# A second tile list ordered by tile number, with the first eight batches gathered and normed inside the expert-tile stage of a two-layer attention and mixture-of-experts kernel

## The chip, the cores and the metric

The kernel runs on one core of one Trainium2 chip. The metric is the device time of one execution in microseconds (us); a kernel is run several times, and the median is compared. The core has a matrix engine (PE; its weight loads are shown as PEld), a vector engine (DVE), a scalar engine with lookup tables (ACT), a general engine (POOL) and a queue engine that issues most transfers (SP). PE writes only to PSUM, which has eight banks of 128 x 512 floats here; everything else works from SBUF, which has 128 partitions.

## The reference, cut to what matters

The input x has 64 batches of 128 tokens of width 128. Two layers follow each other, each an attention and a feed-forward with eight experts:

```
x = x + L0_attention(layernorm(x), fside, ctx)      # 16 heads of width 8; 128 keys from fside and 120 from ctx
x = x + L0_experts(layernorm(x))                    # per token: 8 logits, top 2 experts,
                                                    #   out = sum_k score_k * (silu(a) * g) @ w2[e_k],  a, g = x @ w1[e_k]   (F = 352)
x = x + L1_attention(layernorm(x), ctx)             # 16 heads, 120 keys
x = x + L1_experts(layernorm(x))                    # top 2 of 8 experts, hidden width 64, gelu
```

The token count is 64 x 128 = 8192, so layer 0's experts have 16384 rows of work. The logits of layer 0 depend on the data, so which rows belong to which expert is known only while the kernel runs.

## The kernel before, in words

The whole x stays in SBUF as 16 tiles `xg[g]` of four batches each (a group is GB = 4 batches). There are three stages, one after the other.

Stage 1 is `attention(0, ...)`: a loop over `it`, one new batch per turn, in which a batch's scores, softmax, values and output projection are spread over five turns (so 64 + 5 turns). Beside it the layer-0 router runs (`Router`, called at fixed points of each turn): it norms a group, finds the two experts of each token, and scatters each token's normed row into an array `xs` in HBM, where every expert has its own region of CAP rows, in the order of the tokens. The row that a token got there within all regions is kept in `posns`, the choice of expert as a one-hot in `chosen`.

Stage 2 is `tile_stage`. It works through NTL = 71 tiles of TT = 256 rows of one expert. For each tile, `fetch(t)` reads from a list the expert and the first row into registers of SP (`value`, L851), then issues three transfers (the 256 rows from `xs`, the expert's weights, the scores of the rows). `turn` transposes the rows on PE, `hidden` makes the hidden layer (12 matmul records at L1030, silu on ACT at L1034, product on DVE at L1035), `project` the output (L1043), scales it on DVE (L1049) and writes it from SP into an HBM array `ys` (L1050). Slots rotate over five buffers, and tile t + 3 is fetched while tile t is worked on. `between(t)` puts in small pieces of other work after each tile. There are two lists: "a", for the first NA = 32 tiles, is made when 40 of the 64 batches have been routed, so that stage 2 can begin before the routing is over; "b", for the other 39, is made when all are routed. Both go expert by expert. The generator `lists` makes them, and after them `back`, for every token the two rows of `ys` where its results will stand.

Stage 3 is `attention(1, ...)`. Before it can norm a batch, that batch's two result rows per token must come back from `ys`: `Aside1.fetch` issues two indirect gathers per batch from POOL (L1216), `Aside1.lead` adds them to x on POOL (L1228) and takes the statistics on DVE (L112, L113); POOL then makes the root (`Norm.roots`, L155 to L157) and the normed tile `xn` (L167). In the first turns `prep_batch` transposes one batch at a time (L313), makes its queries (L316, L318), and the score matmuls (L373, and L401 for the second pass) follow; from the second group on `prep_x` (L176) and `prep_q` (L289) do a whole group. `norm_of` makes `xn` of a coming group, and `biased` adds the output bias to x. Four gathers go out in each of the first five turns and two in each later one. Layer 1's experts are in stage 3 as pieces between the turns.

The instructions of PE, ACT, DVE and POOL stand in the order in which the program writes them. SP's transfers are ordered so only in the first turns and from the last two turns of stage 1 on; in the stretch between, a scheduler places them as early as what they depend on allows. Every DMA from SP uses one of eight semaphores in turn, so it waits until the transfer eight before it has landed.

Of the kernel before, what the change touches and what calls it, by code (L numbers as in the profile page):

```python
# [44 lines left out]
def transformer_kernel(ctx, tc, a, out):  # L45
# [186 lines left out]
    def attention(layer, w, norm, first, aside):  # L232
# [5 lines left out]
        with ExitStack() as es:  # L238
# [278 lines left out]
            for it in range(B + 5):  # L517
                def on(back, *steps):
                    b = it - back
                    if 0 <= b < B:  # L520
                        for f in steps:
                            f(b)

                def rounds(*which):
                    ba = it if it < B else None
                    bc = it - 2 if 0 <= it - 2 < B else None
                    for r in which:
                        if ba is not None or bc is not None:
                            round_(ba, bc, r)

                if first and it % GB == 2:
                    norm_of(it // GB + 2)
                if 2 <= it <= B + 1:
                    ps_[it - 2] = work.tile([128, nc_, 4, 512], F32, name="p", tag="p")
                if it % GB == 0 and 0 < it // GB + 1 < NG:
                    if it:
                        loads(it // GB + 1)
                vals = (lambda b: values(b, 0), lambda b: values(b, 1), out1)
                if first:
                    rounds(0, 1)  # L540


                    on(5, out4)
                    on(1, shift)
                    on(5, out5)
                    aside.ahead(it)
                    aside.call(it, mtile)
                    on(3, *vals)
                    if it % GB == 2 and it // GB + 1 < NG:
                        context(it // GB + 1)  # L550
                    prep(it, 0)
                    aside.call(it, mtile)
                    rounds(2, 3)
                    on(4, out3)
                    on(3, out2)
                    prep(it, 1)
                    aside.end(it, work, mtile)
                else:
                    on(3, *vals)
                    rounds(0, 1)  # L560


                    aside.piece(mtile)
                    if it < GB - 1:
                        prep_batch(it + 1)
                    prep(it, 0)
                    on(4, out3)
                    on(3, out2)
                    on(5, out4)
                    aside.call(it, mtile)  # L570
                    prep(it, 1)
                    on(1, shift)
                    on(5, out5)
                    aside.ahead(it)
                    if it == GB - 1 or it > GB and it % GB == 1:
                        norm_of(it // GB + 1)
                    if it == 1:
                        biased(0)
                    if it == GB - 1:
                        prep_x(1)  # L580
                        prep_q(1, 0)
                        prep_q(1, 1)
                    aside.fetch_for(it)
                    aside.call(it, mtile)
                ps_.pop(it - 3, None)
                yield
# [259 lines left out]
        return lists_.tile(shape, dt, name=name, tag=name)  # L846

    TILES = {}

    def value(ap, most):  # L850
        return nc.values_load(  # L851
# [25 lines left out]
    def tile_list(name, n, begin, off):  # L877
# [28 lines left out]
        TILES[name] = te_i, tr_i  # L906
        yield

    def lists():
        while len(filled) < GA // 2:  # L910
            yield
# [13 lines left out]
        in_a, cut = small("in_a", [S, E]), small("cut", [S, 1 + E])  # L925
        nc.vector.tensor_scalar(cut, begin_a, float(NA), None, ALU.min)
        nc.vector.tensor_tensor(in_a, cut[:, 1:], cut[:, :E], ALU.subtract)
        nc.vector.tensor_tensor(nt, nt, in_a, ALU.subtract)
        begin_b = summed(nt, "b")
        yield  # L930
        off, two = small("off_b", [S, E]), small("two", [S, E])
        nc.vector.tensor_tensor(two, in_a, begin_b[:, :E], ALU.subtract)
        nc.vector.scalar_tensor_tensor(off, two, float(TT), first_row, ALU.mult, ALU.add)
        top_i = small("top_i", [1, E], I32)
        nc.vector.tensor_copy(top_i, top[0:1, :])
        TILES["top"] = top_i
        yield
        yield from tile_list("b", NTL - NA, begin_b, off)

        first, more, move = small("first", [S, E]), small("more", [S, E]), small("move", [S, E])  # L940
        nc.vector.scalar_tensor_tensor(first, in_a, float(TT), first_row, ALU.mult, ALU.add)
        nc.vector.scalar_tensor_tensor(move, begin_a[:, :E], float(TT), first_row, ALU.mult, ALU.subtract)

        nc.vector.tensor_tensor(more, two, begin_a[:, :E], ALU.add)
        nc.vector.tensor_scalar(more, more, float(NA), -float(TT), ALU.subtract, ALU.mult)
        for k in range(2):
            got = []
            for n, col in enumerate((first, move, more)):
                yield
                prod, by = small("prod", [S, B, E]), small(f"by_{n}", [S, B])  # L950
                nc.vector.tensor_tensor(
                    prod, chosen[:, k], col.unsqueeze(1).to_broadcast([S, B, E]), ALU.mult
                )
                yield
                nc.vector.tensor_reduce(by, prod, AX.X, ALU.add)
                got.append(by)
            yield
            at_, move_, more_ = got
            nc.vector.tensor_tensor(at_, posns[:, k], at_, ALU.is_ge)
            nc.vector.tensor_tensor(more_, more_, at_, ALU.mult)  # L960
            nc.vector.tensor_tensor(move_, move_, more_, ALU.add)
            nc.vector.tensor_tensor(back[:, :, k], move_, posns[:, k], ALU.add)


    SLOTS = 5

    def tile_stage(work, mtile):


        w_of, x_of, xT_of, hT_of, share_of, y_of = {}, {}, {}, {}, {}, {}  # L970
        probes = [None]
        zeros_left = list(range(E))

        def slot(t):
# [5 lines left out]
            return s.rearrange("p b h i w -> p (b h i w)")  # L980

        def fetch(t):
            name, u = ("a", t) if t < NA else ("b", t - NA)
            te_i, tr_i = TILES[name]
            e = value(te_i[:, u : u + 1], E - 1)
            r = value(tr_i[:, u : u + 1], E * CAP - TT)
            s = slot(t)
            n = NF * 3 * 128
            w = s[:, :n].rearrange("p (c f) -> p c f", c=NF)
# [48 lines left out]
        def project(t):  # L1038
# [8 lines left out]
            y, share = y_of.pop(t), share_of.pop(t)  # L1047
            for h in range(2):
                nc.vector.tensor_scalar(y[:, h, :], po[:, h, :], share[:, h, :], None, ALU.mult)  # L1049
            nc.sync.dma_start(ys[t * TT : (t + 1) * TT].rearrange("(h p) d -> p h d", p=S), y)  # L1050
            probes.append(y[0:1, 0, 0:1])

        def between(t):

# [3 lines left out]
                    rt.call(probes[-1], mtile)  # L1058
            elif zeros_left and "top" in TILES:
                zeros(zeros_left.pop(0))  # L1060
            next(aside0.steps, None)
            if t == NA:
                kvT = work.tile([D, GB, KF], F32, name="kvT", tag="kvT")
                kvT = kvT.rearrange("d b k -> d (b k)")[:, : GB * KC]
                kvT = kvT.rearrange("d (b k) -> d b k", b=GB)
                nc.sync.dma_start(kvT, a["ctxT"][:, 0:GB, :])
                probes[0] = kvT
            if t == NA + 6:
                keys_of(l1, probes[0], 0, KC, mtile())
            if t == NA + 10:  # L1070
                values_of(l1, probes[0], 0, KC, mtile())

        for t in range(2):
# [5 lines left out]
        for t in range(NTL):  # L1079
# [5 lines left out]
            if t + 3 < NTL:  # L1085
                if t + 3 == NA:
                    assert len(filled) == NG // 2 and not zeros_left
                    for _ in aside0.steps:
                        pass
                fetch(t + 3)  # L1090
            if t > 2:
                between(t)
# [14 lines left out]
    class Aside0(Ahead):  # L1107
# [28 lines left out]

        def end(self, it, work, mtile):

            if it == B - 2:
                self.tiles = tile_stage(work, mtile)  # L1140
            if it >= B - 2:
# [37 lines left out]
    wr1 = load_const("wgT", [D, E], a["wgT"])  # L1179
    bg = load_row("bg", E)  # L1180
    lw1 = load_const("lw1T", [D, E * R], a["lw1T"])
    steps256 = load_row("steps256", CAP // TT)
    tiles = load_const("tiles", [1, NTL], a["tiles"])
    select = load_const("select", [128, 4, 128], a["select"])
    lw2 = load_const("lw2T", [128, 4, D], a["lw2T"].rearrange("(c p) d -> p c d", p=128))
    with tc.manual_schedule(engines=ORDERED):
# [7 lines left out]
    class Aside1:  # L1194


        def __init__(self, pool):
            self.pool, self.got, self.b, self.xn = pool, {}, 0, None
            self.xnTs, self.gates, self.ready = {}, [], []
            for k in range(2):  # L1200
                t = pool.tile([S, QM, 32], F32, name=f"gates_{k}", tag=f"gates_{k}")
# [20 lines left out]
        def lead(self, b):  # L1222
# [4 lines left out]
                for k in range(2):  # L1227
                    nc.gpsimd.tensor_tensor(x, x, y[:, k], ALU.add)  # L1228
            norms[2].stats(b)
            if b < GB:  # L1230
                if b % 2:
                    norms[2].roots(b - 1, b + 1)
                    self.xn = norms[2].normed(0, xn=self.xn, js=(b % GB - 1, b % GB))
            elif b % GB == GB - 1:
                norms[2].roots(b + 1 - GB, b + 1)

        def normed(self, j):
# [5 lines left out]

        def ahead(self, it):

            for b in ((2, 3), (), (4, 5), (6, 7), (8, 9), (10, 11))[it] if it < 6 else (it + 6,):
                if b < B:
                    self.lead(b)

        def fetch_for(self, it):  # L1250
            self.fetch(2 if it < 5 else 1)

        def xnT_of(self, g):
            self.xnTs[g] = self.pool.tile([D, GB * S], F32, name="xnT", tag="xnT", bufs=4)
# [74 lines left out]

    with ExitStack() as es:  # L1330
        aside1 = Aside1(es.enter_context(tc.tile_pool(name="yb", bufs=1)))
        aside1.fetch(3)
        aside1.lead(0)
        aside1.lead(1)
        aside1.fetch(1)
        with tc.manual_schedule(engines=ORDERED):
            for _ in attention(1, l1, norms[2], False, aside1):
                pass
# [2 lines left out]
def _laid_out(inp):  # L1341
# [57 lines left out]
    for e in range(E):  # L1399
        t[:, e, e // 2, e % 2, :] = 1.0  # L1400
    o["select"] = t.reshape(128, 4, 128)
    o["tiles"] = np.arange(NTL, dtype=np.float32).reshape(1, -1)
    o["first_row"] = np.arange(E, dtype=np.float32) * CAP
    o["wgT"] = A["L1_ffn_Wg"].T
    o["bg"] = A["L1_ffn_bg"]
# [21 lines left out]
```

## Time and profile before

| what | value |
|---|---|
| median of 3 runs | 1624.24 us (1620.74 to 1625.42) |
| the profiled execution's own time | 1627.08 us |
| its span, first to last instruction | 1625.1 us, mean granted PE clock 0.954 |
| PE busy in 0 to 600 us (stage 1) | about 96 to 99% after the first 100 us |
| PE busy in 640 to 980 us (stage 2) | 310.45 of 340 us |
| PE busy in 980 to 1060 us (start of stage 3) | 49.44 of 80 us, granted clock 0.68 |
| PE busy in 1060 to 1560 us (rest of stage 3, without its end) | about 93% |
| DVE busy in stage 2 | 159.47 of 340 us |
| DMA share in stage 2 | 0.62 of 16 engines, 181 GB/s |

Two views are used most. A table of windows gives for each stretch the busy time of each engine with the number of instructions, then the granted PE clock (1.00 is full speed), the share of the 16 DMA engines that was busy, and the GB/s moved. A list of waits gives, for each engine and line, the engine and line that ended the wait, the total of the waits, how many there were and the longest. In a timeline, a row is start, duration, engine, line, operation and tiles, and in brackets the idle time ahead of it and what ended it.

### The profile page before, as it was taken

The page shows a single profiled execution, that of the slowest core. Times are in us where ns is not written, and L with a number is a line of the kernel's source. Part 1 is how long each engine was busy: PE and PEld are TensorE (multiplying, and loading weights), DVE is VectorE, ACT ScalarE, POOL GpSimd, SP SyncE. Part 2 cuts the span into 40 slices and gives each one's busy share as a digit, 9 for nine tenths or more (in the row PEclk, how much of TensorE's full clock was granted, in tenths as well). Part 3 has the DMA queues.
Part 4 walks back from the last instruction along what each step waited for, and adds up shares of the span by engine and source line. Part 5 has one row for each costly group of instructions (what it writes and reads, how often), then busy time and mean ns, then how long its engine had stood idle before and what let it go on. Part 6 is the DMA issues. An engine that isn't in the chain of part 4 may idle for free.

```text
span 1625.1 us, 44888 instructions
## 1 busy us (share of the span) xinstructions
PE 1489.3 (92%) x18162; PEld 1184.0 (73%) x18162; DVE 1072.5 (66%) x2935; ACT 842.1 (52%) x1739; POOL 642.3 (40%) x1198
## 2 busy tenths in 40 slices
PE   7999999999999998879999994788999999999997
PEld 5777777777777676768888883567777777777775
DVE  6778888888889883545544442477666656667763
ACT  4666666666566564423333332455555555555553
POOL 4123355656565344640000005575554555443200
PEclk9999999999999998999999996799998989899999
DMA  8311122222222211667666651110001111000000
GB/s 211 84 45 45 45 58 60 59 58 74 58 64 71 65 51 59 181 175 207 198 193 189 192 172 43 29 36 25 27 27 36 29 30 30 29 27 15 10 13 26
DMA packets 124129, 123.88 MB, mean 76 GB/s; under 512 B 47123, under 2 KB 106515, under 8 KB 122003
## 3 DMA queue, kind: packets, MB, share of 16 engines
q1 hardware_dynamic: 115730, 103.71, 23.2%
q0 software_dynamic: 8192, 17.32, 3.4%
q8 instruction: 143, 2.34, 0.6%
q14 instruction: 64, 0.52, 0.1%
HBM read 97.31 MB, written 23.67 MB: 74 GB/s over the span
## 4 chain that ended last, share of the span: by engine, by line
PE 74%; DVE 11%; DMA 4%; issue 3%; ACT 3%; POOL 3%; SPq 1%; another core or an unknown queue 0%; POOLq 0%; DVEq 0%; ACTq 0%
PE bank L401 13%; PE bank L373 12%; PE bank L1030 9%; PE bank L446 9%; PE bank L1305 4%; PE bank L1284 3%; DVE nm L385 3%; PE bank L1043 3%; PE bank L289 2%; DMA q<-xs 2%; PE bank L1294 2%; PE bank L482 2%; PE bank L202 2%; PE bank L214 2%; PE bank L653 2%
## 5 line engine op out<-in xcount | busy, mean ns | idle before, releaser
L385 DVE TENSOR_REDUCE nm<-bank 128x2 f32<-128x496 f32 (+1 forms) x768 | 465.2, 663 | 151.0 <-PE bank L401 89.6
L401 PE MATMUL bank<-q,k 32*120 32x256 f32 (+1 forms) x3072 | 480.4, 408 | 16.8 <-issue 5.6
L373 PE MATMUL bank<-k,q 32*128 32x248 f32 (+1 forms) x4096 | 466.0, 345 | 11.1 <-issue 7.5
L409 ACT ACTIVATE p<-bank 120x512 f32<-120x512 f32 (+1 forms) x768 | 402.4, 603 | 138.0 <-PE bank L401 102.8
L373 PEld LDWEIGHTS bank<-k,q 32*128 32x128 f32 x4096 | 355.5, 191 | 80.4 <-issue 32.9
L401 PEld LDWEIGHTS bank<-q,k 32*120 32x120 f32 (+1 forms) x3072 | 302.2, 181 | 47.2 <-DVE nm L385 16.1
L446 PE MATMUL bank<-p,v 128*32 128x128 f32 (+1 forms) x4096 | 178.4, 278 | 4.6 <-DVE nm L385 4.0
L1035 DVE TENSOR_TENSOR p<-p,bank 128x256 f32<-128x256 f32 x213 | 88.2, 420 | 139.5 <-ACT p L1034 126.4
L784 POOL DMA_INDIRECT xs<-xn,at x128 | 129.3, 1010 | 28.5 <-issue 24.9
L455 ACT COPY ov<-bank 128x256 f32<-128x256 f32 x128 | 47.9, 374 | 176.1 <-PE bank L446 130.9
L1216 POOL DMA_INDIRECT yb<-ys,back x128 | 124.0, 968 | 32.2 <-issue 24.6
L1034 ACT ACTIVATE p<-bank 128x256 f32<-128x256 f32 x213 | 80.9, 384 | 102.4 <-PE bank L1030 97.1
L446 PEld LDWEIGHTS bank<-p,v 128*32 128x32 f32 (+1 forms) x4096 | 110.8, 110 | 29.6 <-issue 15.9
L1030 PE MATMUL bank<-q 128*128 128x256 f32 x516 | 122.3, 388 | 3.0 <-ACT oT L477 3.0
L433 DVE SCALAR_TENSOR_TENSOR q<-bank,c_smask,q 128x256 f32<-128x256 f32 x256 | 111.2, 476 | 14.2 <-PE bank L430 10.9
L167 POOL TENSOR_SCALAR xn<-x,mv,rstd 128x128 f32<-128x128 f32 x252 | 110.6, 451 | 6.2
L155 POOL TENSOR_SCALAR rstd<-mv 128x4 f32<-128x4 f32 (+1 forms) x33 | 6.6, 199 | 268.0 <-DVE mv L113 181.2
L293 ACT ACTIVATE q<-bank,c_a_bq,c_hmask 128x512 f32<-128x512 f32 x120 | 87.3, 785 | 47.7 <-PE bank L289 47.7
L1030 PEld LDWEIGHTS bank<-q 128*128 128x128 f32 x516 | 97.4, 196 | 15.6 <-ACT oT L477 3.4
L446 PE MATMUL bank<-p,vc 120*32 120x128 f32 x2048 | 104.2, 272 | 0.5 <-issue 0.5
L1202 POOL MEMSET gates<- 128x256 f32 x2 | 0.6, 312 | 251.3 <-DMA ys<-q 251.3
L138 POOL TENSOR_TENSOR mv<-st 128x4 f32<-128x4 f32 x31 | 6.4, 207 | 195.4 <-DVE st L109 195.4
(205 smaller groups left out, 2412.5 us busy)
## 6 DMA issues: line engine op xcount, KB each, us to landing
q<-in_w SPq DMA_DIRECT2D x43, 576.0 KB
vc<-in_w SPq DMA_DIRECT2D x28, 576.0 KB
vc<-in_ctx_v SPq DMA_DIRECT2D x16, 960.0 KB
k<-in_ctx_k SPq DMA_DIRECT2D x32, 240.0 KB
q<-xs SPq DMA_DIRECT2D x43, 128.0 KB
ys<-q SPq DMA_DIRECT2D x43, 128.0 KB
x<-in_x SPq DMA_DIRECT2D x16, 256.0 KB
kvT<-in_fsideT SPq DMA_DIRECT2D x16, 256.0 KB
```

Of the source, the lines that this page charges most:

```text
L167: nc.gpsimd.tensor_scalar(xn[:, j, :D], xg[g][:, j, :], self.mv[:, b, 0:1], self.rstd[:, b : b + 1], ALU.add, ALU.mult,)
L293: nc.scalar.activation(q4s[g][:, :, s, :], pq.rearrange("p (b q) -> p b q", b=GB), AF.Identity, bias=w["bq"][:, s : s + 1], scale=hmask[:, ...
L373: nc.tensor.matmul(pa[:, u, :], lhsT=q4s[g][r, j, s, :], rhs=k2[g % 2][r, s // 2, j, :], start=True, stop=True,)
L385: nc.vector.tensor_reduce(nm[b % 2].rearrange("q i (a s) -> q a i s", s=16)[:, 2 * ra + v : 2 * ra + v + len(slots) // 2, :, 0], pa.rearra ...
L401: nc.tensor.matmul(pb[:n, v * 256 : (v + 1) * 256], lhsT=k2[g % 2][r, v, j, k0 : k0 + n], rhs=q4s[g][r, j, 2 * v : 2 * v + 2, :].rearrange ...
L409: nc.scalar.activation(ps_[b][:n, c, ra, :], pb[:n], AF.Exp, scale=SCALE)
L433: nc.vector.scalar_tensor_tensor(q, pm, smask[:, v : v + 1], q, ALU.mult, ALU.add)
L446: nc.tensor.matmul(pav[32 * ra : 32 * ra + 32, v * S : (v + 1) * S], lhsT=vs[g % 2][c][:, j, 4 * v + ra, i, :], rhs=p[:n, c, ra, (2 * v + ...
L784: s = nc.gpsimd.indirect_dma_start(xs, bass.IndirectOffsetOnAxis(at[:, j, k : k + 1], 0), xn, None)
L1030: nc.tensor.matmul(ph[:, u, :], lhsT=w[:, c, u * 128 : (u + 1) * 128], rhs=xT, start=True, stop=True)
L1035: nc.vector.tensor_tensor(hT[:, c, :], sa, ph[:, 1, :], ALU.mult)
L1216: nc.gpsimd.indirect_dma_start(y[:, k, b % 2, :], None, ys, bass.IndirectOffsetOnAxis(back[:, b, k : k + 1], 0),)
```

## The change

The change has four parts.

First, list "b" is made in another order: by a tile's number within its expert, then by expert. `tile_list_by_number` works on all 128 partitions at once (264 = 33 x 8 possible tiles per partition), marks those that list "a" left over, numbers them with a scan, and each partition picks out the tile of its own number; so the list stands down the partitions, one tile in each, instead of along one partition. `back` follows the new order by a longer formula.

Second, `first_results` gathers, adds and norms the first eight batches while the last tiles are worked on. The rows of batches 2u and 2u + 1 are within the first 256(u + 1) rows of each expert, so their results stand in `ys` once list "a" and the first 8(u + 1) tiles of list "b" are written. It begins after tile 41, with one step per tile and eight tiles per pair of batches.

Third, stage 3 begins with those two groups normed (`READY`): its gathers start at batch 8, two batches in the first turn and one in each later turn.

Fourth, each of the 71 tiles of `ys` is filled with zeros from SP during stage 1, so that a gather never reads a row that was not written.

Beside these, `between` takes two steps of the list's generator per tile instead of one once list "b" is there, and the keys and values of stage 3's first group are made two and four tiles earlier.

```diff
@@ attention, second layer
-                    if it == GB - 1 or it > GB and it % GB == 1:
+                    if it > GB and it % GB == 1:
                         norm_of(it // GB + 1)
-                    if it == 1:
-                        biased(0)
                     if it == GB - 1:
+                        normed[1] = READY[1]
                         prep_x(1)
@@ lists
+    def tile_list_by_number(s, n):
+        shape = [S, U, E]
...
+        nc.vector.tensor_tensor(one, u, s256.unsqueeze(1).to_broadcast(shape), ALU.is_ge)
+        nc.vector.tensor_tensor(at, n256.unsqueeze(1).to_broadcast(shape), u, ALU.is_gt)
+        nc.vector.tensor_tensor(one, one, at, ALU.mult)
+        nc.vector.tensor_tensor_scan(at_, one_, nothing, 0.0, ALU.add, ALU.add)
+        nc.vector.tensor_tensor(at_, at_, one_, ALU.mult)
+        nc.vector.tensor_scalar(at_, at_, row_number[:, 0:1], None, ALU.is_equal)
...
+        nc.vector.tensor_tensor(one, at, order.unsqueeze(1).to_broadcast(shape), ALU.mult)
+        nc.vector.tensor_reduce(te, one_, AX.X, ALU.add)
+        nc.vector.tensor_tensor(one, at, u, ALU.mult)
+        nc.vector.tensor_reduce(tr, one_, AX.X, ALU.add)
...
+        TILES["b"] = te_i, tr_i
@@ lists(), the rows of back, for each of the two choices k
-            for n, col in enumerate((first, move, more)):
+            for n, col in enumerate((first, move, order)):
                 yield
                 prod, by = ...
                 nc.vector.tensor_tensor(prod, chosen[:, k], col..., ALU.mult)
                 yield
                 nc.vector.tensor_reduce(by, prod, AX.X, ALU.add)
...
+            nc.vector.tensor_tensor(prod, order..., o..., ALU.is_gt)
+            yield
+            nc.vector.tensor_tensor(prod, prod, u.unsqueeze(2).to_broadcast(wide), ALU.add)
+            nc.vector.tensor_tensor(prod, prod, in_a.unsqueeze(1).to_broadcast(wide), ALU.max)
+            yield
+            nc.vector.tensor_tensor(prod, prod, nt.unsqueeze(1).to_broadcast(wide), ALU.min)
+            nc.vector.tensor_reduce(u, prod, AX.X, ALU.add)
...
@@ tile_stage
         def fetch(t):
-            name, u = ("a", t) if t < NA else ("b", t - NA)
+            te_i, tr_i = TILES["a" if t < NA else "b"]
+            u = (slice(0, 1), slice(t, t + 1)) if t < NA else (slice(t - NA, t - NA + 1), slice(0, 1))
...
+        def first_results(t):
+            u, step = divmod(t - NA - E - 1, E)
+            if not 0 <= u < 4:
+                return
+            if step == 0:
+                y = work.tile([D, GB, KF], F32, name="kvT", tag="kvT")
...
+                needed = written[NA : NA + E * (u + 1)]
+                for b in range(2):
+                    for k in range(2):
+                        g = nc.gpsimd.indirect_dma_start(
+                            y[:, k, b, :], None, ys,
+                            bass.IndirectOffsetOnAxis(back[:, 2 * u + b, k : k + 1], 0),
+                        )
...
+                        behind(g, needed)
+            elif step == 1:
...
+                for k in range(2):
+                    nc.gpsimd.tensor_tensor(x, x, y[:, k], ALU.add)
+            elif step == 2:
+                for b in range(2):
+                    norms[2].stats(2 * u + b)
+            elif step == 3 and u % 2:
+                g = u // 2
+                norms[2].roots(g * GB, g * GB + GB)
+                READY.append(norms[2].normed(g))
+            elif step == 4 and u % 2:
+                nc.gpsimd.tensor_tensor(xg[g], xg[g], l1["bo"]..., ALU.add)
...
-            next(aside0.steps, None)
+            for _ in range(2 if "b" in TILES else 1):
+                next(aside0.steps, None)
+            if t == NA + E:
+                for _ in aside0.steps:
+                    pass
+            first_results(t)
...
+            if t == NA + 4:
+                keys_of(l1, probes[0], 0, KC, mtile())
             if t == NA + 6:
-                keys_of(l1, probes[0], 0, KC, mtile())
-            if t == NA + 10:
                 values_of(l1, probes[0], 0, KC, mtile())
@@ Aside0.end, each turn of stage 1
+            for t in range(2 * (it - GB), 2 * (it - GB) + 2):
+                if 0 <= t < NTL:
+                    nc.sync.dma_start(
+                        ys[t * TT : (t + 1) * TT].rearrange("(h p) d -> p h d", p=S), zero[:, :, :D]
+                    )
@@ Aside1
-            self.pool, self.got, self.b, self.xn = pool, {}, 0, None
+            self.pool, self.got, self.b, self.xn = pool, {}, 2 * GB, READY[0]
...
-            for b in ((2, 3), (), (4, 5), (6, 7), (8, 9), (10, 11))[it] if it < 6 else (it + 6,):
+            for b in ((), (8,), (9,), (10,), (11,), ())[it] if it < 6 else (it + 6,):
...
-            self.fetch(2 if it < 5 else 1)
+            self.fetch(2 if it == 0 else 1)
@@ start of stage 3
         aside1 = Aside1(es.enter_context(tc.tile_pool(name="yb", bufs=1)))
-        aside1.fetch(3)
-        aside1.lead(0)
-        aside1.lead(1)
-        aside1.fetch(1)
```

## The prediction

> **What bounds the kernel now.** I read the page first, for where PE loses time.
>
> ```profile
> PE   7999999999999998879999994788999999999997
> POOL 4123355656565344640000005575554555443200
> PEclk9999999999999998999999996799998989899999
> L1202 POOL MEMSET gates<- 128x256 f32 x2 | 0.6, 312 | 251.3 <-DMA ys<-q 251.3
> ```
>
> PE is at nine tenths nearly everywhere; the hole is in the slice from 975 us, where its clock is low too. POOL is empty for some 250 us before it, waiting for `ys` (the row of L1202). So the tiles run at PE's pace, POOL has room in them, and the start of stage 3 is bound by something else. The windows from 930 us on, busy times in the order PE, PEld, DVE, ACT, POOL, SP, then clock, DMA share, GB/s:
>
> ```profile
> 975.00:980.00 5.00, 1.91 (x18) 1.72 (x16) 1.33 (x5) 0.00 (x0) 0.10 (x1) 1.00 0.18 52
> 980.00:985.00 5.00, 0.00 (x0) 0.00 (x0) 0.00 (x0) 0.00 (x0) 3.90 (x6) 0.56 0.43 134
> 995.00:1000.00 5.00, 4.10 (x32) 3.51 (x34) 0.73 (x2) 1.77 (x5) 1.07 (x2) 0.50 0.00 0
> 1030.00:1035.00 5.00, 3.21 (x6) 1.23 (x6) 0.00 (x0) 0.59 (x1) 4.47 (x8) 0.50 0.00 0
> ```
>
> PE stops at 976.9, comes back at 995 at half clock, and POOL is the busy engine between. The chain that ended last gives the order (start, duration, what), the list of waits from 975 to 1070 the totals (total, count, longest):
>
> ```profile
> 976.95 0.62 DVE q L1049 x2
> 977.59 1.83 DMA ys<-q
> 979.89 0.56 POOL gates L1202 x2
> 983.23 2.43 DMA yb<-ys,back
> 994.51 0.45 POOL xn L167
> 995.00 0.49 PE bank L313
> 997.17 3.57 PE bank L373 x29
> ```
> ```profile
> PE bank L313 <- POOL xn L167: 18.1, 1, 18.1
> DVE st L112 <- POOL x L1228: 17.5, 2, 14.3
> PE bank L176 <- POOL xn L167: 5.1, 1, 5.1
> ACT p L409 <- remote: 3.8, 1, 3.8
> ```
>
> One serial path: last write, gathers, sums, statistics, root, `xn`, transposes. PE's waits after it (5.1 at L176) are the same chain for later batches.
>
> **Cost of the zeros.** In the order of the changed program, SP's 71 fills are not spread over stage 1: they stand together, eight behind the second group's kvT, one more kvT, then 63, all ahead of the next group's k, vc and kvT. Before, SP had free time there:
>
> ```profile
> 37.83 1.34 SPq L255 DMA_DIRECT2D kvT<-in_fsideT  x2
> 62.71 0.93 SPq L260 DMA_DIRECT2D k<-in_ctx_k  x2
> 81.65 0.47 PE L373 MATMUL bank<-k,q 32*128 32x248 f32 x1
> ```
>
> These are rows of the timeline; the next is again from the windows.
>
> ```profile
> 70.00:80.00 10.00, 10.00 (x165) 7.65 (x169) 7.83 (x18) 6.27 (x13) 0.00 (x0) 1.00 0.49 121
> ```
>
> In 975 to 980 two writes of this size and shape take a DMA share of 0.18 of 5 us: 0.45 us of all 16 engines each, so 71 take 32 us. Earlier loads are under way until about 48 us (my reading of the DMA shares), so the burst ends near 80 us; k was issued at 62.71 and its data is needed by L373 at 81.65. SP comes free at 76 to 78, and with 6 us for k's transfers k lands near 83: 1.5 to 2 us late. PE is busy 10.00 of 10 us there, so that is carried to the end. Take +2 (0, if 48 us is too late an estimate, to +8).
>
> **Cost in the tiles.** PE needs 4.4 to 4.5 us per tile and nothing may be added to its path. (a) The list's DVE work: list "b" keeps about ten 264-wide operations (0.43 each by L864), as many as before; `back` grows by four 512-wide operations at 0.68 (L951, L955) and some sixteen 64-wide ones at 0.22 in all, about +8 us counting the extra reductions, at most 2.7 us in a tile since `between` takes two steps. DVE is busy 8.10 of 20 us in 940 to 960, but order matters: a piece stands ahead of the next scaled output.
>
> ```profile
> 792.22 0.61 DVE L1049 TENSOR_SCALAR vc<-bank,vc 128x128 f32<-128x128 f32 x2 [0.50 <-PE bank L1043]
> 796.98 0.61 DVE L1049 TENSOR_SCALAR vc<-bank,vc 128x128 f32<-128x128 f32 x2 [0.21 <-PE bank L1043]
> ```
>
> Between these, 3.0 us of list work stood in one tile; they are 4.76 apart instead of 4.45: 0.3 us lost. With three or four such tiles more: +1 (0 to +4). The list's registers come from 39 partitions instead of one; a load took 0.27 or 0.49 us on SP before, and no row shows another partition, so 0 (up to +3: fetches run three tiles ahead).
>
> (b) The 16 gathers, each about 0.97 us plus 0.30 of issue on POOL and 2.4 to land; eight sums at 0.74; roots and xn. POOL is empty, and each step has a tile of 4.45 us: four gathers 5.1 us plus landing, sums two tiles after they were let go, and the statistics (L112 0.28 and L113 0.18 on DVE, four and four per group) come at about 13.8 us with sums done at about 11.2. Their transfers are 16 x 0.21 us of 16 engines (16 packets of 4096 B at 206 ns per engine in the trace), against a share of 0.70. What waits if the cover fails: DVE's statistics hold the next L1035, and with it PE. Here the Trainium skill speaks against the change. The row: a sum takes 0.74 with DVE idle (989.19), and two took 1.54 with DVE at work (1045.12); L1035 takes 0.42 with POOL at work and without. "GPSIMD Engine Reference", "8. Key points", has the vector engine and this engine contend for SBUF, against DVE instructions with two SBUF inputs. Were DVE held for as long as the sums last, that is 8 x 0.74 = 5.9 us; by the row nothing. The list's operations have two SBUF inputs, but L1035 reads one from PSUM. I take +1 for (b) (0 to +4).
>
> **Gain at the start of stage 3.** No gather, sum or `xn` stands ahead of PE now. What remains of waits is ACT's query step behind the last write's landing (977.59 + 1.83, seen by POOL at 979.89). L314 to L373 took 995.51 to 997.17 = 1.66 us. So L373 starts at 979.9 + 1.66 = 981.5 instead of 997.17: **-15.7**. The first rounds are still at half clock: PE is idle from 976.9 to 981.5, 4.6 us; in 722 to 727 an idle of 4.91 us was followed by 0.50. By the Trainium skill, "TensorE: Matmul & The Clock Gate", "Part 1: The HAM clock gate (the \"warmup\" mystery)", about 3.4 us of activity bring full speed back, so only the first round would be slow and a second gain of half of 3.57 = 1.8 us would follow. The trace shows 0.50 for 15 us from 995 with PE busy 4.10, 4.09 and 4.64 of 5. By the rule the sum is 1.8 lower; I go by the row: 0.
>
> **Gain in turns 1 to 6.** Turn 3's `prep_x(1)` waited for its own group's `xn`:
>
> ```profile
> 1031.06 1.77 PE L176 MATMUL bank<-ident,xn 128*128 128x128 f32 x4 [5.05 <-POOL xn L167]
> 1065.57 1.80 PE L289 MATMUL bank<-xnT,c_a_wq 128*128 128x512 f32 x2 [1.58 <-DVE nm L385]
> ```
>
> READY[1] is there from the tiles on: -5.05. Behind it the clock was 0.50 (1030 to 1035); L176 took 1.77 against 0.63 in stage 1 and L289 2.08 against 1.12: -2 more, **-7**. In turns 4 to 6 DVE's L112 waited 3.2 us for POOL's sum at 1064.5 (the rest of the 17.5 above is the 14.3 before turn 1), PE then 1.58, with clocks of 0.54 and 0.66 in two windows. Now one batch per turn is due a turn earlier, and POOL has about 11 us of work for it where two turns give 13: **-4** (-6 to 0). PE also stood from 1013.4 to 1018.6 in turn 2, where ACT and DVE waits of 3.8 and 3.7 are put down to "remote", which names no cause; POOL's gathers are thick there. I count half: **-2.5** (-4.9 to 0).
>
> **Sum.** +2 +1 +1 -15.7 -7 -4 -2.5 = -25.2. The profiled execution took 1627.1 (span 1625.1 and 2.0 around it): 1601.9. It was 2.8 above the median of 1624.24, so 1599. With all costs 0 and every gain in full I get -33, and -37 if the clock stays up: 1587. With costs at +8 +4 +4 +3 and gains of only -12 and -5: +2, 1626.
>
> **The rivals.**
>
> 1. Head only (0.20). Turns 1 to 6 are held by their own start-up (PE at half clock, first groups' ACT and DVE work, the same pieces of layer 1's router) and only the 15.7 comes, less 4 of costs: about -12, 1612. For it: the unexplained "remote" stall, and a clock that was low for reasons other than waits. Against: the 5.05 us at L176 has a named releaser that is gone.
>
> 2. Slower, by the zero burst starving k in stage 1 (0.12). If the fills take twice 0.45 us, because they meet the earlier loads and SP's eight semaphores let each wait for the one eight before, the burst is 64 us, SP comes free near 108, and k lands at 112 instead of by 81.65: +30, and +2 of cold clock after it; with the -27 of the rest, +5: 1629. It decides from a burst of about 57 us, 0.8 us per fill. For it: k, vc and kvT are really queued behind all 63 in SP's order. Against: the share in 975 to 980 gives 0.45, and the DMA share in 50 to 60 us was 0.01, all engines free. Two thirds of this case is slower; the rest lies around no change.
>
> 3. The change doesn't do what it says (0.03): a gather of the tiles waits for every write of `ys`, so nothing moves and the costs stay: +4, 1628. Against: the statistics of the first pair stand on DVE ahead of later tiles' products, so such a wait couldn't be resolved at all; the gathers wait for writes of the first tiles of list "b" only.
>
> **How the numbers follow.** The measurement can tell about 0.3%, 4.9 us, from no change. The forecast holds 0.65 and is all faster (1587 to 1608); of rival 1, 0.18 is faster and 0.02 the same; of rival 2, 0.08 slower, 0.02 same, 0.02 faster; of rival 3, 0.02 slower, 0.01 same. That makes 0.85, 0.05 and 0.10. The range 1589 to 1616 leaves out a few hundredths at the low end, the tail of rival 1, and rivals 2 and 3.
>
> **What would show it.** Right: in the list of waits of the new trace, PE's wait at L313 of about 18 us is gone, and PE's idle before its first L373 of stage 3 is under 6 us; L176 of turn 3 without a wait for POOL; 16 gathers among the tiles, which still run at 4.45 us each; SP's `ys<-zero` ending near 80 us and PE's wait at about turn 8 for k under 3 us. Wrong: an idle of PE of 10 us or more between 80 and 115 us (rival 2); DVE waiting for POOL's sums in the tiles, or tiles above 4.6 us; a stall of 4 us or more again in turns 2 to 6 (rival 1); gathers after the last `ys` write (rival 3).

## The result and the profile after

The changed kernel takes 1600.97 us (median of 4 runs, 1598.49 to 1604.19) against 1622.49 us of the kernel before on the same chip: a ratio of 0.9869, 95% interval 0.9841 to 0.9898, 21.5 us less. The profiled execution took 1601.67 us with a span of 1599.9, against 1627.08 and 1625.1. The forecast was 1599 for the median and 1601.9 for the profiled execution. The total is nearly exact; the terms are not, and it was luck that two errors of some 6 us cancelled.

The page of the changed kernel, its first part:

```profile
PE   7989999999999999888999998988999999999987
POOL 4122255555565535443020302366554544443210
PEclk9999999999999999999999999799999989999999
```

PE's hole near 975 us is gone, and POOL has work in what were its empty slices. The chain that ended last, between the stages (start, duration, what):

```profile
987.49 0.62 DVE q L1104 x2
988.12 1.82 DMA ys<-q
991.99 3.38 PE bank L373 x29
```

From the issue of the last write to the first scores there are now 3.87 us, where there were 19.58: the 15.7 of the sum, to a tenth. But the last output itself comes 10.5 us later than before (987.49 against 976.95). The timeline of SP and of PE says where most of that was lost:

```profile
37.67 9.37 SPq L1247 DMA_DIRECT2D ys<-zero  x8
47.65 39.63 SPq L1247 DMA_DIRECT2D ys<-zero  x63
87.38 1.04 SPq L260 DMA_DIRECT2D k<-in_ctx_k  x2
```
```profile
90.72 0.74 PE L373 MATMUL bank<-k,q 32*128 32x248 f32 x1 [7.10 <-DMA k<-in_ctx_k]
```

The fills keep SP until 87.4 us, k is issued 25 us later than before, and PE stands for 7.10 us. Behind that the clock is low, too:

```profile
88.00:95.00 7.00, 4.28 (x35) 3.62 (x36) 1.77 (x3) 1.56 (x3) 0.00 (x0) 0.51 0.95 223
```

To split the rest I compare the start of DVE's step L433, which stands once in every turn from turn 1 on, and of the scaled output of each tile, in both traces. The last column has the same from two profiles of a later chip, number 13 of the experiments below (the changed kernel there, e5_after, against the kernel with the new list alone, e6_list, which is as fast as the kernel before):

| part | forecast | first chip | chip 13 |
|---|---|---|---|
| stage 1 up to turn 7 | 0 | +1.9 | -1.4 |
| turns 7 and 8 (fills, wait for k) | +2 | +8.7 | +11.2 |
| rest of stage 1 and router's end | 0 | -1.9 | 0 |
| tiles 0 to 53 (list, first eight gathers) | +1 | -0.1 | +1.8 |
| tiles 53 to 70 (last eight gathers) | +1 | +2.0 | +1.6 |
| last tile to first scores | -15.7 | -15.7 | -15.3 |
| from there to L433 of turn 3 | -2.5 | -1.4 | +1.4 |
| turn 3 | -7 | -7.8 | -8.7 |
| turns 4 to 6 | -4 | -9.6 | -4.9 |
| rest of stage 3 | 0 | -1.3 | +2.7 |

Each column adds up to the difference of its two spans, -25.2 and -11.6 (the medians on chip 13 differ by 12.9). On chip 13 both kernels have the list, and 1.7 of the 1.8 us in tiles 0 to 53 fall between tiles 2 and 3, where the first tiles meet the end of the routing; in e8_spread_wait nothing is lost there.

One more reading changes what was measured. POOL's timeline in the tiles, and DVE's scaled output of tile 32, the first tile of list "b":

```profile
817.82 1.00 POOL L1127 DMA_INDIRECT kvT<-ys,back  x1 [80.92 <-DVE p L1090]
826.41 0.95 POOL L1127 DMA_INDIRECT kvT<-ys,back  x1 [0.27 <-POOL x L1139]
```
```profile
818.80 0.61 DVE L1104 TENSOR_SCALAR q<-bank,q 128x128 f32<-128x128 f32 x2 [0.50 <-DMA q<-xs]
```

The first gathers start before the first tile of list "b" has its output, about nine tiles ahead of their place in the program. The instructions of the built kernel say why: the first gather's waits name the writes of tiles 0 to 31 and none of the eight tiles of list "b" that `needed` holds. Those writes are declared to be of no concern to the gathers (`declare_no_dep` with the group "writes"), and the wait that `behind` adds for them is not in the program. So the measured kernel is one whose early gathers wait for list "a" alone.

On this input that does no harm: worked out from the reference's routing, list "a" holds four or five tiles of each of seven experts and one tile of the last, and every row of batches 0 to 7 stands in these 32 tiles. It is luck of the data. With another routing a row of these batches can stand in list "b", and a gather that runs this early would read the zeros of the fill. The experiments e3_wait and e8_spread_wait make the gathers wait.

### The profile page after: what moved, and what is told of

It is laid out like the page before. It is cut to its first block, busy times and chain, and to the rows that moved or that the text cites. A ratio compares the mean times of both kernels' runs of the same rounds, so it can differ in the third digit from the quotient of the medians.

```text
span 1599.9 us, 45004 instructions
## 1 busy us (share of the span) xinstructions
PE 1484.9 (93%) x18162; PEld 1182.0 (74%) x18162; DVE 1084.0 (68%) x2960; ACT 843.9 (53%) x1739; POOL 641.1 (40%) x1195
## 4 chain that ended last, share of the span: by engine, by line
PE 73%; DVE 10%; DMA 4%; issue 3%; SPq 3%; POOL 3%; ACT 3%; another core or an unknown queue 0%; POOLq 0%; ACTq 0%; DVEq 0%
PE bank L401 12%; PE bank L373 12%; PE bank L446 9%; PE bank L1085 9%; PE bank L1413 4%; PE bank L1392 4%; PE bank L1098 3%; DVE nm L385 3%; PE bank L289 2%; SPq L1247 2%; PE bank L1402 2%; PE bank L482 2%; DMA q<-xs 2%; PE bank L214 2%; PE bank L652 2%
## 5 line engine op out<-in xcount | busy, mean ns | idle before, releaser
L409 ACT ACTIVATE p<-bank 120x512 f32<-120x512 f32 (+1 forms) x768 | 403.3, 605 | 140.5 <-PE bank L401 106.0
L373 PE MATMUL bank<-k,q 32*128 32x248 f32 (+1 forms) x4096 | 462.4, 345 | 13.3 <-DMA k<-in_ctx_k 7.1
L373 PEld LDWEIGHTS bank<-k,q 32*128 32x128 f32 x4096 | 351.8, 191 | 81.6 <-issue 36.3
L155 POOL TENSOR_SCALAR rstd<-mv 128x4 f32<-128x4 f32 x32 | 6.3, 198 | 384.9 <-DVE mv L113 296.4
L433 DVE SCALAR_TENSOR_TENSOR q<-bank,c_smask,q 128x256 f32<-128x256 f32 x256 | 111.4, 477 | 12.7 <-PE bank L430 11.9
L1328 POOL DMA_INDIRECT yb<-ys,back x112 | 108.8, 971 | 27.7 <-issue 20.1
L293 ACT ACTIVATE q<-bank,c_a_bq,c_hmask 128x512 f32<-128x512 f32 x120 | 87.4, 787 | 45.3 <-PE bank L289 45.2
L1085 PE MATMUL bank<-vc 128*128 128x256 f32 x336 | 77.2, 379 | 0.0
```

Source lines behind the costliest of these rows:

```text
L293: nc.scalar.activation(q4s[g][:, :, s, :], pq.rearrange("p (b q) -> p b q", b=GB), AF.Identity, bias=w["bq"][:, s : s + 1], scale=hmask[:, ...
L373: nc.tensor.matmul(pa[:, u, :], lhsT=q4s[g][r, j, s, :], rhs=k2[g % 2][r, s // 2, j, :], start=True, stop=True,)
L409: nc.scalar.activation(ps_[b][:n, c, ra, :], pb[:n], AF.Exp, scale=SCALE)
L433: nc.vector.scalar_tensor_tensor(q, pm, smask[:, v : v + 1], q, ALU.mult, ALU.add)
L1085: nc.tensor.matmul(ph[:, u, :], lhsT=w[:, c, u * 128 : (u + 1) * 128], rhs=xT, start=True, stop=True)
L1328: nc.gpsimd.indirect_dma_start(y[:, k, b % 2, :], None, ys, bass.IndirectOffsetOnAxis(back[:, b, k : k + 1], 0),)
```

## The experiments

They ran in three sets on three later chips (record numbers 9 for e1 to e4, 13 for e5 to e8, 6 for e9 to e11), which agree closely: the kernel before takes 1537 to 1539 us on them (medians of 11 to 17 runs). The texts of the expectations call them the second or the faster chip. Each ratio is to the kernel before on the run's own chip, so runs of different sets are compared by their ratios. The later chips granted more clock (mean 0.978 in the profile of e6_list, 0.954 for the kernel before on the first chip); what else makes them 5% faster was not followed up.

**The changed kernel on a later chip.** 

> The changed kernel itself once more, so that the other runs of this set have it on their own chip. Theory A (the prediction's mechanisms, independent of the chip): 0.9869 of before, as measured. Rival B (part of the gain hangs on the clock that this chip grants in stage 3): 0.990 to 0.992, as the kernel with xn made in turn 3 gave on the faster chip.

Ratio 0.9903 (0.9885 to 0.9920), 1523.25 us: 13.6 us less than before, where the first chip had 21.5. That is what rival B named: part of the gain depends on the chip. That is likely rather than shown, since this interval overlaps the end of the first chip's (0.9841 to 0.9898). The table has the difference in turns 4 to 6, the later turns and the fills. That the clock makes it, as rival B says, is not shown.

**The fills alone.** One loop added to the kernel before:

```
         def end(self, it, work, mtile):
+            for t in range(2 * (it - GB), 2 * (it - GB) + 2):
+                if 0 <= t < NTL:
+                    nc.sync.dma_start(ys[t * TT : (t + 1) * TT]..., zero[:, :, :D])
```

> The kernel before with the 71 fills added at the same place in the program, nothing else changed. Theory A (the fills alone cost what stage 1 lost): 8 to 11 us more than before, with a wait of PE for k of about 7 us near 84 us and SP free near 87 us. Rival B (the 8.5 us are from the other new loads and their order): 2 us more or less.

Ratio 1.0084 (1.0061 to 1.0108): 11 us more than before, at the upper end of theory A. The list of waits has it in one line (total, count, longest):

```profile
PE bank L373 <- DMA k<-in_ctx_k: 9.9, 1, 9.9
```

The 63 fills take 37.91 us of SP here, and k is issued at 88.50. So the loss belongs to the fills alone.

**The fills spread.**

```
+            if 0 <= 2 * (it - GB) < NTL:
+                nc.gpsimd.memset(zero[0:1, 0, 0:1], 0.0)
```

> The changed kernel with its 71 fills held back: a one-element memset of the zero tile on POOL, once a turn, lets two fills go per turn instead of 71 in one burst. Theory A (the burst alone delays k of the third group): PE's wait for k near 84 us goes, and with it the 8.5 us lost in turn 7; 8 to 10 us less than the changed kernel. Rival B (the loss only moves: two fills in each turn meet k, vc and kvT of that turn): 3 us less or nothing.

Ratio 0.9828 (0.9801 to 0.9856), 1510.6 us: by the ratios 11.5 us less than the changed kernel, a little over the 8 to 10 of theory A, as the loss is larger on these chips (11 us in e2_fillonly). No wait for k is in its list of waits from 60 to 120 us. The same 9.3 MB cost nothing that can be seen when they are not in one burst.

**Fewer fills, still in one burst.** `if 0 <= t` becomes `if NA <= t`, so 39 fills.

> The changed kernel with only the 39 fills of list b's tiles, still in one burst ahead of the third group's k. Theory A (the loss is the length of the burst against k's due time): at the measured 0.63 us per fill SP is free near 67 us, k lands near 73 us, ahead of its use near 82 us, and the wait is wholly gone, as with the fills spread: 10 to 12 us less than the changed kernel. Rival B (the loss is in proportion to the bytes): 4 to 6 us less.

Ratio 0.9842 (0.9815 to 0.9870), 1512.46 us: 9.4 us less than the changed kernel by the ratios, 10.8 by the medians. Loss in proportion to bytes would have given back under half. SP's timeline:

```profile
40.10 30.81 SPq L1247 DMA_DIRECT2D ys<-zero  x38
71.02 1.04 SPq L260 DMA_DIRECT2D k<-in_ctx_k  x2
```

SP is free at 71.0 instead of the expected 67 (among its first fills SP stands for 4.2 us, and two issues there take 1.8 and 1.5), k is issued 11 us before its use, and PE has no wait for it. The loss begins only where the burst overruns k's due time.

**The list alone.** The changed kernel without fills and `first_results`, and with stage 3's start as before.

> The kernel before with list b by number, its longer back and two steps of it per tile, and the keys made earlier; no fills, no early gathers, the start of stage 3 as before. Theory A (the prediction's step: DVE's list work is hidden but for about 1 us): 0 to 2 us more than before. Rival B (the tiles of 0 to 30, where the list is made, are what the changed kernels lost 3 to 4 us in on the second chip): 3 to 5 us more, in tiles 3 to 30.

Ratio 0.9998 (0.9986 to 1.0009). Theory A, at its low end: DVE's longer list work is hidden, within 2 us.

**Gathers that wait.** The gathers' `declare_no_dep` and `behind` and the writes' group are taken out:

```
-            if t >= NA:
-                tc.add_to_no_dep_group("writes", w.ins)
...
-                        tc.declare_no_dep(g.ins, group="writes", reason="other tiles")
-                        behind(g, needed)
```

> The changed kernel, but the gathers of batches 0 to 7 wait for all tiles of ys written so far in the program (up to tiles 40, 48, 56 and 64), where the built program's gathers wait for tiles 0 to 31 alone and so run from 818 us on. Theory A (POOL has the room, but the sums then come after the place of their statistics in DVE's order, two tiles behind the gathers): DVE waits 2 to 4 us for POOL in each of the four pairs and PE with it, 6 to 14 us more than the changed kernel. Rival B (as the prediction had it, sums at 11.2 us and statistics at 13.8): within 2 us of it.

Ratio 0.9935 (0.9913 to 0.9957), 1527.76 us: 4 to 5 us more than the changed kernel, between both theories. Its list of waits from 835 to 972 us:

```profile
DVE st L112 <- POOL x L1135: 11.9, 4, 3.3
```

As theory A said, DVE waits for POOL's sums in each of the four pairs, about 3 us; but of the 11.9 us less than half reaches the end. From tile 40 to tile 70 the profile takes 133.7 us, where e4_turn3 and e5_after, with the gathers as built, take 131.3 and 131.6.

**Fills spread, gathers that wait, statistics one tile later** (`step == 2` becomes 3 for the statistics, 3 becomes 4 and 4 becomes 5 for what follows).

> The changed kernel with the fills spread (two per turn), the gathers waiting for all tiles of ys written so far, and statistics, roots, xn and bias one tile later. Theory A (with the statistics a tile later the sums are done first, so real waits cost 1 us or less): 11 to 13 us less than the changed kernel. Rival B (the waits cost the 3 to 4 us that they cost with the statistics in their old place): 8 to 9 us less.

Ratio 0.9840 (0.9817 to 0.9863), 1513.08 us: 10 us less than the changed kernel, between both theories. DVE's wait for the sums is gone from the list of waits. Against the spread fills with the gathers as built it is 2 us more by the ratios, with overlapping intervals: what real waits cost lies within the noise, some 4 us at most. Its interval lies below that of the changed kernel: this version beats both kernels and has waits for the writes, so it is the one to build on.

**xn of the second group in turn 3.**

```
-                    if it > GB and it % GB == 1:
+                    if it == GB - 1 or it > GB and it % GB == 1:
                         norm_of(it // GB + 1)
-                        normed[1] = READY[1]
```

> The changed kernel, but xn of the second group is not made among the tiles: POOL makes it in turn 3 of stage 3, just ahead of prep_x(1), as before; its gathers, sums, statistics and roots stay among the tiles. Theory A (having xn early is what took PE's 5.05 us at L176 away): 4 to 7 us more than the changed kernel, with a wait of L176 for POOL. Rival B (the wait was for late gathers, statistics and roots, which are early here; xn alone takes POOL 1.8 us): 0 to 2 us more.

Ratio 0.9906 (0.9880 to 0.9932) against 0.9903: no difference. PE has no wait for POOL at L176, because POOL, with the inputs at hand, makes `xn` 8 us before PE needs it:

```profile
985.60 1.73 POOL L167 TENSOR_SCALAR xn<-x,mv,rstd 128x128 f32<-128x128 f32 x4
```
```profile
995.75 0.60 PE L176 MATMUL bank<-ident,xn 128*128 128x128 f32 x4
```

Theory A falls: what PE had waited for was the chain of gathers, sums, statistics and roots of that group, not `xn`.

**One group instead of two.** `first_results` for u of 0 and 1 only; batches 4 to 7 on the old schedule.

> The changed kernel with only batches 0 to 3 gathered, added and normed among the tiles; batches 4 to 7 come in stage 3 on the schedule of before. Theory A (the head and the later turns are separate terms): the 15 us between the last tile and the first scores stay gained, the waits of POOL's sums and of L176 in turns 3 to 6 are back: 9 to 11 us more than the changed kernel. Rival B (the waits of turns 3 to 6 came from POOL being late with the first group): 3 us more or less.

Ratio 0.9976 (0.9959 to 0.9992), 1532.88 us: 9.6 us more than the changed kernel by the medians, 11.2 by the ratios. Theory A: the waits are back, as the list of waits from 970 to 1050 us has it:

```profile
PE bank L176 <- POOL xn L167: 5.0, 1, 5.0
DVE st L112 <- POOL x L1340: 3.2, 1, 3.2
```

Against the changed kernel, the profile loses 7.8 us in turn 3 and 4.7 us in turns 5 and 6, and nothing in turns 1 and 2 (both need 13.7 us from L433 of turn 1 to that of turn 3).

**Keeping PE busy in the hole.** In `prep_batch`, stage 3, j = 0, ahead of the ACT copy:

```
+                    warm = mtile()
+                    for _ in range(2):
+                        nc.tensor.matmul(warm, lhsT=ident, rhs=select..., start=True, stop=True)
```

> The changed kernel with two more matmuls of 128x512 on PE (results unused) behind the first transpose of stage 3, in the 2.4 us in which PE waits for ACT there. Theory A (the clock falls because PE stands in that hole): the granted clock stays at 1.00 from 985 to 1015 instead of 0.50, and the first turns are 3 to 6 us shorter. Rival B (the clock falls because the first turns are never wholly busy, whatever stands in the hole): the clock falls all the same, 0 to 1 us longer.

Ratio 0.9903 (0.9882 to 0.9924), the same as without. The windows of this kernel (busy PE, PEld, DVE, ACT, POOL, then clock, DMA share, GB/s):

```profile
970.00:975.00 5.00, 3.62 (x21) 2.04 (x21) 0.01 (x1) 1.77 (x5) 2.20 (x4) 1.00 0.42 128
975.00:980.00 5.00, 4.10 (x45) 3.50 (x47) 2.35 (x4) 1.77 (x5) 3.47 (x5) 0.67 0.21 57
980.00:985.00 5.00, 4.64 (x28) 3.03 (x23) 2.45 (x4) 1.83 (x6) 3.94 (x5) 0.50 0.14 39
```

The windows of the changed kernel on the same chip:

```profile
965.00:970.00 5.00, 2.38 (x20) 2.02 (x18) 1.49 (x5) 0.00 (x0) 0.00 (x0) 0.99 0.17 52
970.00:975.00 5.00, 3.87 (x33) 3.58 (x34) 0.98 (x2) 1.77 (x5) 3.87 (x6) 0.50 0.42 126
```

In the kernel without the extra matmuls the clock falls at 969.9, 2.8 us after the last tile's scaled output; here it falls at 976.7, 7.3 us after it. So it holds through the first round of scores, which takes 2.32 us instead of 3.57, and falls all the same, though PE's longest idle in that stretch is 0.8 us. The profile gains about 3 us up to turn 3, but started later for other reasons, and the medians show nothing. Rival B's time came, and theory A falls. Put on top of the spread fills and real waits:

> The kernel with spread fills and real waits, and the two extra matmuls of PE behind the first transpose of stage 3. Theory A (the extra matmuls keep the clock up for the first round, and that is kept): 2 to 4 us less than without them (ratio 0.984). Rival B (when the clock falls is a matter of the phase, and on average nothing is gained): the same within 1.5 us.

Ratio 0.9829 (0.9805 to 0.9854) against 0.9840 (0.9817 to 0.9863): the intervals overlap, and whether it brings 2 us or nothing stays open.

## Why the prediction was right, and where not

**The fills: right place, wrong size.** +2 was taken, +8.7 measured, just over its range. That SP's queue holds k behind all 63 fills, and that PE then waits at L373, came as written; the due time of 81.65 was right too (83.6 in the changed kernel, whose stage 1 runs 1.9 us late). The step that failed is the pace: 0.45 us was the time for which a single fill keeps all 16 engines busy, and the sum took it for the time from one fill to the next. In the burst that time was 39.63 / 63 = 0.63 us, and from 60 to 80 us the engines' share was about 0.7. What SP does in it is in the rows of the fills, and of 43 of the 71 writes of `ys` in the kernel before (ns, shortest, median and longest issue):

```profile
L1247 SPq DMA_DIRECT2D ys<-zero x71: 360/503/1923, 37.7 to 86.8; - x71
L1050 SPq DMA_DIRECT2D ys<-q x43: 360/372/414, 648.1 to 977.6; - x43
```

One issue occupies SP for 0.50 us, and 0.05 lie between two. The 63 issues take 36.5 of the 39.63 us; five of them, of 0.9 to 1.9 us, make the difference from 0.55 to 0.63. So SP was issuing nearly all the time, and its issue, not the engines' work, is the longer of the two prices. Why an issue takes 0.50 us in the burst and 0.37 alone is open. Rival 2's reason, the wait for the transfer eight before, is not what sets this pace: in e2_fillonly and e9_fills39 a fill lands after 2.0 to 2.1 us in the median, and eight fills take 5. Rival 2's mechanism, at 1.4 instead of twice the price per fill, cost 8.7 us, 11.2 on chip 13: the wait of 7.1 (9.0 on chip 13), and the rest fits the low clock behind it, which only rival 2 had counted. The kernel stayed well ahead.

**The tiles.** The list: +1 predicted, nothing measured (e6_list). The gathers: +1 predicted, +1.6 to +2.0 measured for the last eight, 1.5 of it from tile 53 to tile 56, where they run while PE waits for rows of `xs`. That they cause that wait is not shown: with the same gathers, e4_turn3 and e9_fills39 need 13.5 and 13.4 us for this stretch, the changed kernel on chip 13 14.6, and the list alone 13.2. Had the contention between POOL and DVE (the Trainium skill, "GPSIMD Engine Reference", "8. Key points", which gives no size) held DVE for as long as the sums last, it would have cost 5.9 us; the tiles have no room for that.

**The head.** -15.7 predicted and measured. The clock was taken from the row, no gain: in the changed kernel it was 0.50 from 995 to 1015 again. It stayed there even while the profile has PE busy without a break:

```profile
1005.00:1010.00 5.00, 5.00 (x49) 4.22 (x49) 2.58 (x6) 4.30 (x7) 2.63 (x3) 0.50 0.10 28
```

The rule of full speed after about 3.4 us of sustained activity (the Trainium skill, "TensorE: Matmul & The Clock Gate", "Part 1: The HAM clock gate (the "warmup" mystery)") does not foretell this row, as far as a busy PE in the profile is activity in the rule's sense. With the hole filled the clock still fell, with PE busy 3.62 and 4.10 of 5 us. What decides it was not found.

**Turn 3.** -7 predicted, -7.8 and -8.7 measured: L176 stands without a wait and takes 0.60 us instead of 1.77.

```profile
1019.33 0.60 PE L176 MATMUL bank<-ident,xn 128*128 128x128 f32 x4
```

But the reason lies one link further up the chain: not that `xn` is ready, but that its inputs are (e4_turn3 against e10_onegroup).

**Turns 4 to 6.** -4 predicted; -4.9 on chip 13, and taking the second group back gives back 4.7 (e10_onegroup). The step had these waits right. On the first chip it is -9.6, 6.0 of it in turn 4 (1042.2 to 1053.0 in the kernel before), where two other things stand, in the list of waits and in the windows:

```profile
ACT ov L455 <- remote: 4.6, 1, 4.6
```
```profile
1045.00:1050.00 5.00, 4.35 (x38) 3.26 (x36) 2.14 (x4) 2.21 (x5) 1.57 (x3) 0.54 0.05 13
1050.00:1055.00 5.00, 5.00 (x76) 3.78 (x76) 2.73 (x11) 2.42 (x6) 0.00 (x0) 0.78 0.02 5
```

From the two clocks, half speed lasted 4.6 + 2.2 = 6.8 us, worth at most 3.4. The step named the clock of 0.54 without a price and this wait not at all, and how the 6.0 divides between them is open. The changed kernel has waits put down to "remote" as well, in other places (7.0 at DVE's L656, 5.3 at ACT's L409), and none of the eleven profiles of the later chips has one. So that the kernel before had them just here, and not the changed one, looks like chance of the first chip's profiles.

**Turns 1 and 2.** -2.5 was counted for a wait put down to "remote". From L433 of turn 1 to that of turn 3 the first chip needs 14.4 us instead of 17.0, just that much less, and 1.2 of it are lost again ahead of turn 1. But the number is luck. On chip 13 the old start has no such wait and needs less for these turns than the changed kernel, 12.3 us against 13.7. The guess that POOL's crowding caused the wait falls: e10_onegroup, with other gathers in these turns, needs 13.7 as well. What these turns take follows the time for which the clock is half in them:

| half clock in turns 1 and 2, us | the two turns, us | profiles |
|---|---|---|
| 1.0 | 10.95 | e8_spread_wait |
| 3.9 | 12.0 | e4_turn3 |
| 4.8 to 5.0 | 12.3 | e3_wait, e6_list, e7_warm, e9_fills39 |
| 8.7 to 8.9 | 13.6 to 13.7 | e1_spread, e5_after, e10_onegroup, e11_warm2 |
| 9.8 | 14.2 | e2_fillonly |
| 10.4 | 14.4 | the changed kernel, first chip |
| 4.6 | 17.0 | the kernel before, first chip |

Only the last row is out of line, by about 4.7 us, and it is the only one with waits put down to "remote" in these turns. So on the first chip a stall of that size went away, by chance as far as the other profiles show, and a longer half clock took part of it back.

So the forecast of 1599 against 1601 is better than its steps: costs of 10.5 us instead of 4, and gains of 35.7 instead of 29.2, of which 4.7, the excess of turns 4 to 6 over chip 13, came with the first chip alone. That the two differences met is luck. Rival 1, the head only, falls with e10_onegroup: the waits of turns 3, 5 and 6 come back with the old schedule of the second group, and their time with them. Rival 3 falls, but so does the sentence against it: the gathers wait for fewer writes than it said, not more.

## What to carry to other kernels

Price a burst in a queue by its end, and compare that with the due time of the first load behind it. The pace is not the engines' busy time of one transfer alone: look also how long the issuing engine needs for one issue, and take the longer (here 0.55 to 0.63 against 0.45 us). Before the due time a burst of fills cost nothing here, past it the wait counted in full and the low clock behind it came on top, so spreading or halving the burst brought all of it back. When a stall is to go, name which link of the chain is late, not the last one; and read from the instructions or the trace which writes a moved gather waits for, since an order that the code states may not be in the program, and a right result on one input does not show that it is.

## What the runs showed of the hardware

Fills of 128 KB in a row took 0.60 to 0.63 us each (e2_fillonly, the changed kernel) against 0.45 us of engine time; SP needed 0.50 us to issue one. The clock at the start of stage 3 is half for 41.0 and 34.1 us in the two profiles of the later chips that have the old start (e2_fillonly, e6_list), and for 13.7 to 23.9 us in the nine in which the first group is normed early, with a filled hole (13.7, 20.5) as without. Waits put down to "remote" stand in both profiles of the first chip and in none of the later ones. The same change gave 21.5 us on the first chip and 13.6 on chip 13.
